# Adding expert results to the tokens' rows in DRAM, and transposing expert rows on VectorE, in an attention and mixture-of-experts block

## The chip, the cores and the metric

The kernel runs on one core of a Trainium2 chip. The metric is the device time of one execution in microseconds (us), as the median of several runs. The engines named below are TensorE (PE), VectorE (DVE), ScalarE (ACT), GpSimd (POOL) and SyncE (SP); SP, ACT and POOL also issue the DMAs.

## The reference

All tensors are float32. The input x has 4 batches of 512 tokens of 512 features, the context 4 batches of 1024 rows.

```python
def reference(x, ctx, Wq, Wg, bg, Wkv, Wo, Wr, We, be):
    # linear attention, 16 heads of 32 features, f(t) = t + 1 if t > 0 else exp(t)
    h = layernorm(x)
    q, gate = f(h @ Wq.T), sigmoid(h @ Wg.T + bg)
    k, v = split(ctx @ Wkv.T, 2);  k = f(k)
    kv, ks = einsum('bhsd,bhse->bhde', k, v), k.sum(over s)
    attn = einsum('bhld,bhde->bhle', q, kv) / (einsum('bhld,bhd->bhl', q, ks) + 1e-6)
    x = x + (attn * gate) @ Wo.T
    # mixture of experts: 8 experts, the best 2 for each token
    h = layernorm(x)
    w, sel = top_k(h @ Wr, 2);  w = softmax(w)
    gate[token, sel] = w                      # 0 for the other experts
    return x + sum over e of gate[..., e] * (h @ We[e] + be[e])
```

## The kernel before

The four batches go through attention one after another. While the projections of one batch run, the context tiles of the next are turned into keys and values (`kv_tiles`), so that TensorE has work throughout. All rows are tiles of 128 partitions.

After attention, `choose(b)` normalizes the four tiles of a batch into rows of `ROW` = 514 floats (512 features, the home row of the token, and the rank of its first expert), computes the routing logits and finds the two best experts. `dispatch(b)` counts the tokens of each expert and scatters each token's row twice into a DRAM tensor `stream`, which has one region for each expert. Each of the eight scatters of a batch (line 516) is an indirect DMA of GpSimd. `apart` tells the framework that scatters of a group need not wait for each other.

The rows of one expert are then read from `stream` in tiles of 128 tokens. A list says which expert and which rows tile j has; lists are computed on VectorE (`spans`, `listed`) and read into registers. The first 17 tiles (`EARLY`) are full of tokens of batches 0 to 2 and run beside the attention of batch 3; 18 more (`SURE`) always follow, and up to 4 come under a condition, which is not met here: 35 tiles run. `dispatch(3)` stands after the tenth early tile.

In `run`, `rows(j)` loads tile j (line 643, one DMA of 257 KB from SyncE), transposes it with four TensorE transposes (line 89) into PSUM, and ScalarE copies it back (line 231). `expert(j)` multiplies it by the expert's weights (line 86, tile `pe`), VectorE adds the bias into `y` (line 670), and GpSimd scatters `y` to the rows of a DRAM tensor `result` (line 681), where each of a token's two choices has a row of its own. So these scatters go under `apart`, too. `y` has three buffers, and tile j + 1 is loaded and transposed while tile j is multiplied.

At the end `fetch` reads the two result rows of each token back, `add` multiplies them by the gates and adds them to x in SBUF on VectorE (line 817), and `store` writes the output from ScalarE's queue. This is spread over the late tiles by a table of steps, `at_step`: batches 0 and 1 can be read once 8 late tiles are done (`DONE_2`), batch 2 after 14 (`DONE_3`), batch 3 at the end.

Order: the framework places instructions on each engine by when it expects them to be ready. `keep_in_program_order` fixes the order of matmuls and of some DMAs on their engines. It adds waits for what touches the same tensor, unless they are declared independent; a wait stands in the queue of the engine that issues, with all later work of that engine behind it.

Of the kernel before, what the change touches and what calls it, by code (L numbers as in the profile page):

```python
# [31 lines left out]
ROW = D + 2  # L32
# [16 lines left out]
def xattn_moe_kernel(  # L49
# [20 lines left out]
    xpool = ctx.enter_context(tc.tile_pool(name="x", bufs=B * NT))  # L70
# [11 lines left out]
    result = dram.tile([2 * TOK + LATE * P, F], F32, name="result")  # L82
# [8 lines left out]

    def load(dst, src):
        tc.keep_in_program_order(nc.sync.dma_start(out=dst, in_=src))

    def load_ctx(b, s):
        t = cpool.tile([P, ROW], F32, tag="cT", name=f"cT_{b}_{s}")
        t = t[:, 0:D].rearrange("p (c n) -> p c n", n=P)
        load(t, cT[b, s])
        return t
# [14 lines left out]
    bg_sb = wpool.tile([P, NC], F32, name="bg_sb")  # L114
    we_sb = wpool.tile([P, E, NC, F], F32, name="we_sb")

    ctx_tiles = {}

    first = cpool.tile([P, ROW], F32, tag="cT", name="cT_0_0")
    ctx_tiles[0, 0] = first[:, 0:D].rearrange("p (c n) -> p c n", n=P)  # L120
# [72 lines left out]
    home = numbers("home", [[2 * P, B * NT]], [P, B * NT], channel=2)  # L193
# [3 lines left out]
    nc.gpsimd.memset(empty[:, D : D + 1], float(2 * SLOTS))  # L197
    unread = numbers("unread", [[P, LATE]], [P, LATE], base=2 * TOK, channel=1)
# [88 lines left out]
    def kv_tiles(b, lo, hi, between=None, inside=None):  # L287
        for s in range(lo, hi):
            nxt = (b, s + 2) if s + 2 < NS else (b + 1, s + 2 - NS)
            if nxt[0] < B and nxt != (0, 2):  # L290
                ctx_tiles[nxt] = load_ctx(*nxt)
            if b in (1, 2) and s % 2 == 0:
                e = (b - 1) * E // 2 + s // 2
                load(we_sb[:, e], we[e])
            if (b, s) == (3, 0):
                load(stream[SLOTS : SLOTS + P, :], empty)
            if s == 0:
                sums[b] = pkv.tile([P, NC, 2 * P], F32, tag="kvs", name="kvs")
            k = made.pop(s) if s in made else keys(b, s)
            if (b, s) == (0, 0):  # L300
                made[1] = keys(0, 1)
            if inside is not None and s == lo:
                inside()
            v = values(b, s)
            if s > 0:
                kv_add(sums[b], s - 1, *pending[b])
            pending[b] = k, v
            if between is not None:
                between(s - lo)
# [91 lines left out]
    written = {"stream": [], "result": []}  # L401
# [17 lines left out]
    gates = const.tile([P, B * NT, 2], F32, name="gates")  # L419
# [5 lines left out]
    read_back = []  # L425
# [4 lines left out]
    def choose(b, mv, rstd):  # L430

        pl = pmm.tile([P, NT, E], F32, tag="mm", name="pl")
        rows, xTs = [], []
        for t in range(NT):
            row = work.tile([P, ROW], F32, tag="row", name="row", bufs=NT)
            normalize(row[:, 0:D], xs[b][t], t, mv, rstd)
            nc.gpsimd.tensor_copy(row[:, D : D + 1], home[:, b * NT + t : b * NT + t + 1])
            rows.append(row)
# [11 lines left out]
        for t in range(NT):  # L450
            xTs.append(work.tile([P, NC, P], F32, tag="z", name="x2T"))
            transposed(xTs[t], rows[t])
# [22 lines left out]
        routed[b] = rows, m1, hot1, first, m2, hot2  # L475
        yield

    def dispatch(b):

        rows, m1, hot1, first, m2, hot2 = routed.pop(b)  # L480
# [32 lines left out]
        for t in range(NT):  # L513
            nc.vector.tensor_copy(rows[t][:, D + 1 : D + 2], first[:, t, :])
            for i in range(2):
# [3 lines left out]
                    in_=rows[t],  # L519
# [6 lines left out]


        e2 = small.tile([P, NT, 1], F32, tag="e2", name="e2")
        w1 = gates[:, ts(b, NT), 0:1]
        nc.vector.tensor_tensor(e2, m2, m1, ALU.subtract)  # L530
        nc.scalar.activation(e2, e2, AF.Exp)
        nc.vector.tensor_scalar(w1, e2, 1.0, None, ALU.add)
        nc.vector.reciprocal(w1, w1)
        nc.vector.tensor_tensor(gates[:, ts(b, NT), 1:2], e2, w1, ALU.mult)
# [94 lines left out]
    def run(lists, lo, n, early):  # L629
# [3 lines left out]
        def rows(j):  # L633

            row = nc.values_load(
# [3 lines left out]
            if j % 5 < 3:  # L639
                xg = cpool.tile([P, ROW], F32, tag="cT", name="xg")  # L640
            else:
                xg = kvpool.tile([P, ROW], F32, tag="v", name="xg", bufs=2)
            load = nc.sync.dma_start(out=xg, in_=stream[ds(row, P), :])
            if early:
                behind(load, written["stream"][: 2 * NT * (B - 1)], "tokens of the tile")
                early_loads.append(load)
                for put in scatters.get(B - 1, []):
                    tc.declare_no_dep(load.ins, put.ins, reason=full_already)
            else:
                behind(load, written["stream"], "tokens of the tile")  # L650
            xT = work.tile([P, NC, P], F32, tag="qT", name="xgT", bufs=NC)
            transposed(xT, xg)
            return xT, xg

        def expert(j, xT, xg):
# [5 lines left out]
            for c in range(NC):  # L661
# [7 lines left out]
            y = kvpool.tile([P, F], F32, tag="k", name="y")  # L669
# [3 lines left out]
            home_i = small.tile([P, 1], U32, tag="to", name="to", bufs=8)  # L673

            at = small.tile([P, 1], F32, tag="at", name="at", bufs=8)
            nc.gpsimd.tensor_scalar(
                at, xg[:, D + 1 : D + 2], ranked[:, j : j + 1], xg[:, D : D + 1],
                ALU.is_equal, ALU.add,
            )
            nc.gpsimd.tensor_scalar(home_i, at, unread[:, j : j + 1], None, ALU.min)  # L680
            put = nc.gpsimd.indirect_dma_start(  # L681
                out=result,
                out_offset=bass.IndirectOffsetOnAxis(ap=home_i, axis=0),
                in_=y,
                in_offset=None,
            )
            apart(put, "result", "each choice has a row; rows without a token go unread")
            for got in read_back:
                tc.declare_no_dep(put.ins, got.ins, reason="no token of these is in the tile")

        ready = rows(lo)
        for j in range(lo, n):
            cur, ready = ready, rows(j + 1) if j + 1 < n else None
            expert(j, *cur)
# [8 lines left out]
    for b in range(B):  # L703
# [10 lines left out]
        if not more:  # L714
# [15 lines left out]
            early = run(early_list, 0, EARLY, True)  # L730
        product = products(qTs, z, aT)
# [52 lines left out]
    for e in range(E):  # L784
        row = nc.values_load(
            ends[0:1, e : e + 1], [ET.SP], min_val=0, max_val=SLOTS - P,
            skip_runtime_bounds_check_because="a region has room for all tokens",
        )
        fill = nc.sync.dma_start(out=stream[ds(row, P), :], in_=empty)
# [5 lines left out]
    flat = result[0 : 2 * TOK, :].rearrange("(t p i) f -> p t i f", p=P, i=2)  # L795
    homes = [(wpool, "wq"), (wpool, "wg"), (wpool, "wo"), (big, "xT"), (big, "aT")]
    fetched = {}

    def fetch(q, tiles):

        pool, tag = homes[q % len(homes)]
        yt = pool.tile([P, 2, 2, F], F32, tag=tag, name=f"y_{q}")
        for u in range(2):
            load = nc.sync.dma_start(out=yt[:, u], in_=flat[:, 2 * q + u])  # L804
            tc.keep_in_program_order(load)
            behind(load, written["result"][: EARLY + tiles], "results of the tokens")
            for put in written["result"][EARLY + tiles :]:
                tc.declare_no_dep(load.ins, put.ins, reason="no token of these is in the tile")
            read_back.append(load)
            fetched[2 * q + u] = yt[:, u]  # L810

    def add(t):
        xt = xs[t // NT][t % NT]
        yt = fetched[t]
        for i in range(2):
            tc.keep_in_program_order(
                nc.vector.scalar_tensor_tensor(  # L817
                    xt, yt[:, 1 - i, :], gates[:, t, i : i + 1], xt, ALU.mult, ALU.add
                )
            )  # L820

    def store(t):
        tc.keep_in_program_order(
            nc.scalar.dma_start(out=out[t // NT, t % NT], in_=xs[t // NT][t % NT])
        )

    at_step = {}
    first, last = 2 * NT, (B - 1) * NT
    for q in range(first // 2):
        at_step.setdefault(DONE_2 + 2 + q, []).append((fetch, q, DONE_2))  # L830
    for q in range(first // 2, last // 2):
        at_step.setdefault(DONE_3 + 2, []).append((fetch, q, DONE_3))
    for t in range(last):
        step = min(DONE_2 + 3 + t, SURE - 1 - (last - 5 - t) // 2)
        at_step.setdefault(step, []).append((add, t))
        at_step.setdefault(max(step + 1, DONE_2 + 5), []).append((store, t))

    def also(j):
        for what, *of in at_step.pop(j, []):
            what(*of)  # L840

    for j, _ in enumerate(run(late_list, 0, SURE, False)):
        also(j)
# [5 lines left out]
    with tc.If(many > SURE):  # L849
        for _ in run(late_list, SURE, SURE + 1, False):  # L850
            pass
        with tc.If(many > SURE + 1):
            for _ in run(late_list, SURE + 1, LATE, False):
                pass
    for j in sorted(at_step):
        also(j)
    for q in range(last // 2, TOK // P // 2):
        fetch(q, LATE)
    for t in range(last, TOK // P):
        add(t)  # L860
        store(t)
# [43 lines left out]
```

## Time and profile before

| what | value |
|---|---|
| median of 3 runs | 634.57 us (634.34 to 635.91) |
| profiled execution | 633.87 us |
| its span | 632.1 us |
| TensorE busy | 601.8 us, 95% of the span |
| VectorE, ScalarE, GpSimd busy | 235.9, 135.5, 108.5 us |
| mean granted TensorE clock | 0.984 |
| moved by DMA | 70.50 MB, 112 GB/s over the span |
| first and last scatter of a result | 457.58 and 613.52 us |

The span runs from the first to the last instruction of one execution taken by the hardware profiler; the time of that execution has some 1.8 us more. Engine rows give busy time. A group's row has its line, engine and operation, what it writes and reads, its number, its busy time and mean duration, and after the bar the idle time ahead of it and what ended that. A timeline row has start and duration in us, and in brackets the idle time before and its releaser. A DMA's landing is counted from its issue.

### The profile page before, as it was taken

To read this page: it belongs to the slowest core of one execution; us is meant where nothing else is said; L and a number is where in the kernel's file an instruction comes from. 1 tells how busy PE (TensorE), PEld (TensorE's weight loads), DVE (VectorE), ACT (ScalarE), POOL (GpSimd) and SP (SyncE) were. 2 spreads that over 40 slices of the span, in tenths; PEclk is the share of its full clock that TensorE was granted. 3 is DMA by queue.
4 is the path that set the end of the run, shared out by engine and by line. 5 is a ranking of instruction groups with operands and counts; after the bars stand their busy time and mean duration, and the time that the engine had idled before them with its cause. 6 is when DMAs were issued, how large, how long until landed. Compare 5 with 4: busy or idle time off the path is not lost. (4 is left out here: it accounts for less than half of the span.)

```text
span 632.1 us, 6250 instructions
## 1 busy us (share of the span) xinstructions
PE 601.8 (95%) x2044; PEld 300.1 (47%) x2044; DVE 235.9 (37%) x562; ACT 135.5 (21%) x215; POOL 108.5 (17%) x244
## 2 busy tenths in 40 slices
PE   7999999999999999999999999999999999999950
PEld 3555543544564345455543544664444654444420
DVE  3122244126234421622534135149424272111583
ACT  1322222113322122042222114322211221111100
POOL 3100000000005000000230000005331354743420
PEclk9999999999999999999999999999999999999985
DMA  8611300320243023022130100033431279647768
GB/s 316 184 34 54 130 0 7 112 83 18 85 165 117 18 83 109 9 98 89 48 116 18 34 17 17 1 133 135 117 117 33 84 217 238 212 135 255 286 256 284
DMA packets 27808, 70.50 MB, mean 112 GB/s; under 512 B 4288, under 2 KB 4800, under 8 KB 26368
## 3 DMA queue, kind: packets, MB, share of 16 engines
q1 hardware_dynamic: 19536, 48.04, 23.6%
q0 software_dynamic: 5360, 17.60, 7.7%
q10 hardware_dynamic: 2880, 4.46, 1.9%
q8 instruction: 17, 0.28, 0.2%
q14 instruction: 15, 0.12, 0.1%
HBM read 45.93 MB, written 24.16 MB: 111 GB/s over the span
## 5 line engine op out<-in xcount | busy, mean ns | idle before, releaser
L86 PE MATMUL pe<-we_sb,xgT 128*128 x280 | 125.8, 593 | 0.5 <-ACT xgT L231 0.5
L86 PE MATMUL pk<-wkv_sb,cT 128*128 128x512 f32 x256 | 117.8, 604 | 4.1 <-DMA wkv_sb<-in_wkv_dram 4.1
L86 PE MATMUL pv<-wkv_sb,cT 128*128 128x512 f32 x256 | 115.2, 594 | 0.0
L86 PEld LDWEIGHTS pv<-wkv_sb,cT 128*128 128x128 f32 x256 | 48.5, 190 | 62.2 <-issue 59.7
L206 DVE TENSOR_SCALAR ex<-pk 128x512 f32<-128x512 f32 x32 | 22.0, 689 | 147.4 <-PE pk L86 147.4
L86 PEld LDWEIGHTS pe<-we_sb,xgT 128*128 128x128 f32 x280 | 50.7, 190 | 52.1 <-issue 51.1
L86 PEld LDWEIGHTS pk<-wkv_sb,cT 128*128 128x128 f32 x256 | 47.5, 193 | 57.0 <-issue 50.1
L263 POOL MEMSET v<- 128x4 f32 x32 | 3.3, 104 | 344.7 <-PE kvs L86 281.8
L207 ACT ACTIVATE ex<-ex 128x512 f32<-128x512 f32 x48 | 30.2, 629 | 135.4 <-DVE ex L206 128.7
L86 PE MATMUL pg<-xT,wg_sb 128*128 128x512 f32 x128 | 56.7, 596 | 0.0
L86 PE MATMUL pq<-xT,wq_sb 128*128 128x512 f32 x128 | 56.6, 596 | 0.0
L670 DVE TENSOR_TENSOR y<-pe,be_sb 128x512 f32<-128x512 f32 x35 | 24.1, 690 | 85.2 <-PE pe L86 68.8
L86 PE MATMUL po<-wo_sb,aT 128*128 128x512 f32 x128 | 55.6, 592 | 0.0
L231 ACT COPY xgT<-pt 128x512 f32<-128x512 f32 x35 | 20.3, 585 | 120.2 <-PE pt L89 120.2
L681 POOL DMA_INDIRECT result<-y,to x35 | 37.4, 1069 | 36.7 <-DVE y L670 29.9
L516 POOL DMA_INDIRECT stream<-row,slot x32 | 32.1, 1002 | 49.6 <-DVE cmp L544 22.5
L86 PEld LDWEIGHTS kvs<-v,k 128*128 128x128 f32 x256 | 33.3, 191 | 13.4 <-issue 13.2
L86 PEld LDWEIGHTS pg<-xT,wg_sb 128*128 128x128 f32 x128 | 24.0, 190 | 32.0 <-issue 32.0
L86 PEld LDWEIGHTS po<-wo_sb,aT 128*128 128x128 f32 x128 | 24.1, 190 | 29.1 <-issue 28.9
L86 PEld LDWEIGHTS pq<-xT,wq_sb 128*128 128x128 f32 x128 | 23.8, 191 | 27.2 <-issue 27.2
L86 PE MATMUL kvs<-v,k 128*128 128x129 f32 x256 | 34.0, 275 | 0.0
L264 ACT COPY v<-pv 128x512 f32<-128x512 f32 x32 | 18.7, 584 | 53.5 <-PE pv L86 53.5
(151 smaller groups left out, 442.5 us busy)
## 6 DMA issues: line engine op xcount, KB each, us to landing
xg<-stream SPq DMA_DIRECT2D x35, 257.0 KB, 2.8
we_sb<-in_we_dram SPq DMA_DIRECT2D x8, 1024.0 KB, 5.0
y<-result SPq DMA_DIRECT2D x16, 512.0 KB, 7.3
cT<-in_cT_dram SPq DMA_DIRECT2D x31, 256.0 KB, 2.6
x<-in_x_dram SPq DMA_DIRECT2D x16, 256.0 KB, 4.2
out_dram<-x ACTq DMA_DIRECT2D x16, 256.0 KB, 2.8
stream<-empty SPq DMA_DIRECT2D x9, 257.0 KB, 6.9
wkv_sb<-in_wkv_dram SPq DMA_DIRECT2D x8, 256.0 KB, 4.6
```

The source lines that it names most:

```text
L86: tc.keep_in_program_order(nc.tensor.matmul(**operands))
L206: nc.vector.tensor_scalar(ex, src, 0.0, None, ALU.min)
L207: nc.scalar.activation(ex, ex, AF.Exp)
L231: nc.scalar.copy(dst, pt)
L263: nc.gpsimd.memset(v[:, :, P : P + 1], 1.0)
L264: nc.scalar.copy(v[:, :, 0:P], pv.rearrange("p (g f) -> p g f", f=P))
L516: put = nc.gpsimd.indirect_dma_start(out=stream, out_offset=bass.IndirectOffsetOnAxis(ap=slots[i][:, t, :], axis=0), in_=rows[t], in_offse ...
L670: nc.vector.tensor_tensor(y, pe, be_sb[:, ds(no, 1), :].rearrange("p o f -> p (o f)"), ALU.add)
L681: put = nc.gpsimd.indirect_dma_start(out=result, out_offset=bass.IndirectOffsetOnAxis(ap=home_i, axis=0), in_=y, in_offset=None,)
```

## The change

Seven things are done.

- The row of a token carries four extra floats in place of two: its token number, the rank of its first expert, the gate of the second and the difference of the two gates. The gates are computed in `choose` instead of `dispatch`. The four rows of a batch share one tile.
- `result` is replaced by `total`, a DRAM tensor with one row for each token and a tile of spare rows. `choose` stores x after attention there, from ScalarE's queue; x then has 8 tiles in SBUF instead of 16.
- After the bias, ScalarE multiplies `y` by the gate of each token. GpSimd scatters `y` with an addition onto the rows of `total`. These scatters are not declared independent of one another.
- The output leaves by DMA from `total` to the output tensor: batches 0 and 1 after late tile 11, batch 2 after late tile 17, batch 3 at the end in four parts on two queues.
- Rows of an expert are loaded by four DMAs, each of which puts 128 features of all 128 tokens on 32 partitions, and a fifth for the four extra floats. VectorE transposes the tile in 32x32 blocks. The expert weights are laid out to match, so each expert's weights come in four DMAs.
- Loads run five tiles ahead and transposes three; `y` has seven buffers.
- The eight fills behind the streams are issued by ScalarE instead of SyncE.

```diff
-ROW = D + 2
+ROW = D + 4
-    xpool = ctx.enter_context(tc.tile_pool(name="x", bufs=B * NT))
+    xpool = ctx.enter_context(tc.tile_pool(name="x", bufs=2 * NT))
-    result = dram.tile([2 * TOK + LATE * P, F], F32, name="result")
+    total = dram.tile([TOK + P, D], F32, name="total")
...
+    we_rows = we.rearrange("e (c f) i n -> e i f c n", f=HD)
...
-                load(we_sb[:, e], we[e])
+                for i in range(NC):
+                    load(we_sb[ts(i, HD), e], we_rows[e, i])
...
-        rows, xTs = [], []
+        rows = work.tile([P, NT, ROW], F32, tag="row", name="rows", bufs=1)
+        xTs = []
         for t in range(NT):
...
+            normalize(rows[:, t, 0:D], xs[b][t], t, mv, rstd)
+            token = (b * NT + t) * P
+            tc.keep_in_program_order(
+                nc.scalar.dma_start(out=total[token : token + P, :], in_=xs[b][t])
+            )
...
-            load = nc.sync.dma_start(out=xg, in_=stream[ds(row, P), :])
...
+            rows_of = stream[ds(row, P), :]
+            parts = []
+            for i in range(NC):
+                parts.append(
+                    (
+                        xg[ts(i, HD), :].rearrange("t (j f) -> t j f", j=NC),
+                        rows_of[:, ts(i, P)].rearrange("(j t) f -> t j f", t=HD),
+                    )
+                )
+            parts.append((of, rows_of[:, D:ROW]))
+            for dst, src in parts:
+                load = nc.sync.dma_start(out=dst, in_=src)
...
-            transposed(xT, xg)
...
+            nc.gpsimd.tensor_scalar(
+                weight, of[:, 1:2], ranked[:, j : j + 1], of[:, 3:4], ALU.is_equal, ALU.mult
+            )
+            nc.gpsimd.tensor_tensor(weight, weight, of[:, 2:3], ALU.add)
+            token = small.tile([P, 1], U32, tag="token", name="token", bufs=8)
+            nc.gpsimd.tensor_scalar(token, of[:, 0:1], unread, None, ALU.min)
+            xT = work.tile([P, NC, P], F32, tag="xgT", name="xgT", bufs=NC)
+            latest["turn"] = nc.vector.transpose(
+                xT.rearrange("p c (j t) -> p j c t", t=HD),
+                xg.rearrange("p (j c f) -> p j c f", j=NC, f=HD),
+            )
...
-            y = kvpool.tile([P, F], F32, tag="k", name="y")
+            tag, bufs = ("k", 3) if j % 7 < 3 else ("y", 4)
+            y = kvpool.tile([P, F], F32, tag=tag, name="y", bufs=bufs)
...
+            nc.scalar.activation(y, y, AF.Copy, scale=weight)
             put = nc.gpsimd.indirect_dma_start(
-                out=result,
-                out_offset=bass.IndirectOffsetOnAxis(ap=home_i, axis=0),
+                out=total,
+                out_offset=bass.IndirectOffsetOnAxis(ap=token, axis=0),
                 in_=y,
                 in_offset=None,
-            )
-            apart(put, "result", "each choice has a row; rows without a token go unread")
-            for got in read_back:
+                compute_op=ALU.add,
+            )
+            added.append(put)
+            for got in finished:
                 tc.declare_no_dep(put.ins, got.ins, reason="no token of these is in the tile")
...
+        def ahead(j):
+            if j + 5 < n:
+                with tc.issue_after(latest["load"].ins) if latest else nullcontext():
+                    loaded.append(rows(j + 5))
+            if j + 3 >= lo and loaded:
+                ready.append(turned(j + 3, *loaded.pop(0)))
+
+        for j in range(lo - 5, lo):
+            ahead(j)
+        yield
         for j in range(lo, n):
-            cur, ready = ready, rows(j + 1) if j + 1 < n else None
-            expert(j, *cur)
+            ahead(j)
+            with tc.issue_after(latest["turn"].ins):
+                expert(j, *ready.pop(0))
             yield
...
-        fill = nc.sync.dma_start(out=stream[ds(row, P), :], in_=empty)
+        fill = nc.scalar.dma_start(out=stream[ds(row, P), :], in_=empty)
...
+    def leave(b, queue, parts=1):
+        n = L // parts
+        for i in range(parts):
+            r = slice(b * L + i * n, b * L + (i + 1) * n)
+            done = queue[i % len(queue)].dma_start(
+                out=out[b].rearrange("t p d -> (t p) d")[i * n : (i + 1) * n], in_=total[r, :]
+            )
+            tc.keep_in_program_order(done)
+            finished.append(done)
+        latest["load"] = done
+
+    late = run(late_list, 0, SURE, False)
+    next(late)
+    for j, _ in enumerate(late):
+        if j == DONE_2 + 3:
+            leave(0, [nc.sync])
+            leave(1, [nc.sync])
+        if j == DONE_3 + 3:
+            leave(2, [nc.sync])
...
+    leave(B - 1, [nc.sync, nc.scalar], 4)
```

`DONE_2` is 8, `DONE_3` is 14 and `SURE` is 18.

More of the change, by code (lines that the diff above doesn't have):

```diff
@@ L1 @@
-from contextlib import ExitStack
+from contextlib import ExitStack, nullcontext
 import concourse.bass as bass
@@ L89, in transpose @@
         tc.keep_in_program_order(nc.tensor.transpose(dst, src, ident))
+    latest = {}
     def load(dst, src):
-        tc.keep_in_program_order(nc.sync.dma_start(out=dst, in_=src))
+        latest["load"] = nc.sync.dma_start(out=dst, in_=src)
+        tc.keep_in_program_order(latest["load"])
     def load_ctx(b, s):
-        t = cpool.tile([P, ROW], F32, tag="cT", name=f"cT_{b}_{s}")
-        t = t[:, 0:D].rearrange("p (c n) -> p c n", n=P)
+        t = cpool.tile([P, NC, P], F32, tag="cT", name=f"cT_{b}_{s}")
         load(t, cT[b, s])
@@ L115, in xattn_moe_kernel @@
     we_sb = wpool.tile([P, E, NC, F], F32, name="we_sb")
+    we_rows = we.rearrange("e (c f) i n -> e i f c n", f=HD)
     ctx_tiles = {}
-    first = cpool.tile([P, ROW], F32, tag="cT", name="cT_0_0")
-    ctx_tiles[0, 0] = first[:, 0:D].rearrange("p (c n) -> p c n", n=P)
+    ctx_tiles[0, 0] = cpool.tile([P, NC, P], F32, tag="cT", name="cT_0_0")
     for half in range(2):
@@ L191, in numbers @@
         return t
-    home = numbers("home", [[2 * P, B * NT]], [P, B * NT], channel=2)
+    home = numbers("home", [[P, B * NT]], [P, B * NT], channel=1)
     empty = const.tile([P, ROW], F32, name="empty")
     nc.gpsimd.memset(empty, 0.0)
-    nc.gpsimd.memset(empty[:, D : D + 1], float(2 * SLOTS))
-    unread = numbers("unread", [[P, LATE]], [P, LATE], base=2 * TOK, channel=1)
+    nc.gpsimd.memset(empty[:, D : D + 1], float(SLOTS))
+    unread = numbers("unread", [[0, 1]], [P, 1], base=TOK, channel=1)
     expert_no = numbers("expert_no", [[0, GROUPS], [1, E]], [P, GROUPS, E])
@@ L293, in kv_tiles @@
                 e = (b - 1) * E // 2 + s // 2
-                load(we_sb[:, e], we[e])
+                for i in range(NC):
+                    load(we_sb[ts(i, HD), e], we_rows[e, i])
             if (b, s) == (3, 0):
                 load(stream[SLOTS : SLOTS + P, :], empty)
+                load(total[TOK : TOK + P, :], empty[:, 0:D])
             if s == 0:
@@ L398, in attention_out @@
             nc.vector.tensor_tensor(xs[b][t], po, xs[b][t], ALU.add)
-    written = {"stream": [], "result": []}
+    written = {"stream": []}
     def apart(dma, group, why):
@@ L417, in behind @@
             )
-    gates = const.tile([P, B * NT, 2], F32, name="gates")
     seen = {0: const.tile([P, E], F32, name="seen")}
@@ L424, in xattn_moe_kernel @@
     early_loads = []
-    read_back = []
+    added, finished = [], []
     full_already = "the tile is full of tokens of other batches"
@@ L432, in choose @@
         pl = pmm.tile([P, NT, E], F32, tag="mm", name="pl")
-        rows, xTs = [], []
+        rows = work.tile([P, NT, ROW], F32, tag="row", name="rows", bufs=1)
+        xTs = []
         for t in range(NT):
[L435 to L438, printed above, removed]
+            normalize(rows[:, t, 0:D], xs[b][t], t, mv, rstd)
[3 more added lines that the diff above has]
+            )
+        nc.gpsimd.tensor_copy(
+            rows[:, :, D : D + 1], home[:, ts(b, NT)].rearrange("p (t o) -> p t o", o=1)
+        )
         def logits(t):
@@ L451, in choose @@
             xTs.append(work.tile([P, NC, P], F32, tag="z", name="x2T"))
-            transposed(xTs[t], rows[t])
+            transposed(xTs[t], rows[:, t, :])
             if t > 0:
@@ L473, in choose @@
         m2, hot2, _ = largest("2")
-        routed[b] = rows, m1, hot1, first, m2, hot2
+        e2 = small.tile([P, NT, 1], F32, tag="e2", name="e2")
+        w1 = small.tile([P, NT, 1], F32, tag="w1", name="w1")
+        nc.vector.tensor_tensor(e2, m2, m1, ALU.subtract)
+        nc.scalar.activation(e2, e2, AF.Exp)
+        nc.vector.tensor_scalar(w1, e2, 1.0, None, ALU.add)
+        nc.vector.reciprocal(w1, w1)
+        nc.vector.tensor_copy(rows[:, :, D + 1 : D + 2], first)
+        nc.vector.tensor_tensor(rows[:, :, D + 2 : D + 3], e2, w1, ALU.mult)
+        nc.vector.tensor_tensor(
+            rows[:, :, D + 3 : D + 4], w1, rows[:, :, D + 2 : D + 3], ALU.subtract
+        )
+        routed[b] = rows, hot1, hot2
         yield
     def dispatch(b):
-        rows, m1, hot1, first, m2, hot2 = routed.pop(b)
+        rows, hot1, hot2 = routed.pop(b)
         both = small.tile([P, NT, E], F32, tag="both", name="both")
@@ L513, in dispatch @@
         for t in range(NT):
-            nc.vector.tensor_copy(rows[t][:, D + 1 : D + 2], first[:, t, :])
             for i in range(2):
@@ L518, in dispatch @@
                     out_offset=bass.IndirectOffsetOnAxis(ap=slots[i][:, t, :], axis=0),
-                    in_=rows[t],
+                    in_=rows[:, t, :],
                     in_offset=None,
@@ L525, in dispatch @@
                 scatters[b].append(put)
[L528 to L534, printed above, removed]
     def per_expert(name):
@@ L639, in rows @@
             if j % 5 < 3:
-                xg = cpool.tile([P, ROW], F32, tag="cT", name="xg")
+                xg = cpool.tile([P, D], F32, tag="cT", name="xg")
             else:
-                xg = kvpool.tile([P, ROW], F32, tag="v", name="xg", bufs=2)
-            load = nc.sync.dma_start(out=xg, in_=stream[ds(row, P), :])
[L644 to L650, printed above, removed]
@@ L651, in rows @@
-            xT = work.tile([P, NC, P], F32, tag="qT", name="xgT", bufs=NC)
-            transposed(xT, xg)
-            return xT, xg
-        def expert(j, xT, xg):
+                xg = kvpool.tile([P, D], F32, tag="v", name="xg", bufs=2)
+            of = small.tile([P, ROW - D], F32, tag="of", name="of", bufs=8)
+            rows_of = stream[ds(row, P), :]
[7 more added lines that the diff above has]
+                )
@@ new lines, in rows @@
+            parts.append((of, rows_of[:, D:ROW]))
+            for dst, src in parts:
+                load = nc.sync.dma_start(out=dst, in_=src)
+                latest["load"] = load
+                if early:
+                    behind(load, written["stream"][: 2 * NT * (B - 1)], "tokens of the tile")
+                    early_loads.append(load)
+                    for put in scatters.get(B - 1, []):
+                        tc.declare_no_dep(load.ins, put.ins, reason=full_already)
+                else:
+                    behind(load, written["stream"], "tokens of the tile")
@@ new lines, in rows, with turned @@
+            return xg, of
+        def turned(j, xg, of):
+            weight = small.tile([P, 1], F32, tag="weight", name="weight", bufs=8)
+            nc.gpsimd.tensor_scalar(
[9 more added lines that the diff above has]
+            )
+            return xT, weight, token
@@ L656, in expert @@
+        def expert(j, xT, weight, token):
             no = nc.values_load(
@@ L672, in expert @@
             )
[L673 to L678, printed above, removed]
-            )
-            nc.gpsimd.tensor_scalar(home_i, at, unread[:, j : j + 1], None, ALU.min)
+            nc.scalar.activation(y, y, AF.Copy, scale=weight)
             put = nc.gpsimd.indirect_dma_start(
-                out=result,
-                out_offset=bass.IndirectOffsetOnAxis(ap=home_i, axis=0),
+                out=total,
+                out_offset=bass.IndirectOffsetOnAxis(ap=token, axis=0),
                 in_=y,
                 in_offset=None,
+                compute_op=ALU.add,
             )
-            apart(put, "result", "each choice has a row; rows without a token go unread")
-            for got in read_back:
+            added.append(put)
+            for got in finished:
                 tc.declare_no_dep(put.ins, got.ins, reason="no token of these is in the tile")
-        ready = rows(lo)
+        loaded, ready = [], []
+        def ahead(j):
[7 more added lines that the diff above has]
+        yield
         for j in range(lo, n):
-            cur, ready = ready, rows(j + 1) if j + 1 < n else None
-            expert(j, *cur)
+            ahead(j)
+            with tc.issue_after(latest["turn"].ins):
+                expert(j, *ready.pop(0))
             yield
@@ L730, in xattn_moe_kernel @@
             early = run(early_list, 0, EARLY, True)
+            next(early)
         product = products(qTs, z, aT)
@@ L785, in xattn_moe_kernel @@
         row = nc.values_load(
-            ends[0:1, e : e + 1], [ET.SP], min_val=0, max_val=SLOTS - P,
+            ends[0:1, e : e + 1], [ET.Activation], min_val=0, max_val=SLOTS - P,
             skip_runtime_bounds_check_because="a region has room for all tokens",
         )
-        fill = nc.sync.dma_start(out=stream[ds(row, P), :], in_=empty)
+        fill = nc.scalar.dma_start(out=stream[ds(row, P), :], in_=empty)
         apart(fill, "stream", "rows behind the last token of a stream")
@@ L792, in xattn_moe_kernel @@
             tc.declare_no_dep(fill.ins, load.ins, reason="behind all tokens of the stream")
[L795 to L819, printed above, removed]
-            )
[L822 to L840, printed above, removed]
@@ L842, in xattn_moe_kernel @@
-    for j, _ in enumerate(run(late_list, 0, SURE, False)):
-        also(j)
+    def leave(b, queue, parts=1):
[4 more added lines that the diff above has]
+                out=out[b].rearrange("t p d -> (t p) d")[i * n : (i + 1) * n], in_=total[r, :]
+            )
+            tc.keep_in_program_order(done)
+            finished.append(done)
+        latest["load"] = done
@@ L849, in xattn_moe_kernel @@
     with tc.If(many > SURE):
+        latest.clear()
         for _ in run(late_list, SURE, SURE + 1, False):
@@ L852, in xattn_moe_kernel @@
         with tc.If(many > SURE + 1):
+            latest.clear()
             for _ in run(late_list, SURE + 1, LATE, False):
                 pass
[L855 to L861, printed above, removed]
+    leave(B - 1, [nc.sync, nc.scalar], 4)
 def kernel(**inputs):
```

## The prediction

> **What bounds the kernel now.** I read the page first, for the engine that sets the time, then the groups by line and shape, TensorE's timeline of the expert stage, GpSimd's timeline of the same stage, the scatter's own line, and the chain that ended last.
>
> ```profile
> PE 601.8 (95%) x2044; PEld 300.1 (47%) x2044; DVE 235.9 (37%) x562; ACT 135.5 (21%) x215; POOL 108.5 (17%) x244
> ...
> q0 software_dynamic: 5360, 17.60, 7.7%
> ...
> xg<-stream SPq DMA_DIRECT2D x35, 257.0 KB, 2.8
> ...
> result<-y,to POOLq DMA_INDIRECT x35, 3.6
> ```
>
> TensorE is busy for 95% of the span, so work taken off it counts, unless something else takes its place. A scatter lands 3.6 us (median) after its issue. The scatters' queue q0 takes 7.7% of the span on each DMA engine: 0.077 x 632.1 / 67 scatters (35 + 32) = 0.73 us of moving data per scatter; the rest of the 3.6 us is fixed.
>
> TensorE in the late stage, one expert tile after another:
>
> ```profile
> 571.05 0.60 PE L89 MATMUL pt<-ident,xg 128*128 128x128 f32 x4
> 571.49 3.60 PE L86 MATMUL pe<-we_sb,xgT 128*128 x8
> 574.92 0.60 PE L89 MATMUL pt<-ident,xg 128*128 128x128 f32 x4
> 575.36 3.60 PE L86 MATMUL pe<-we_sb,xgT 128*128 x8
> ```
>
> The period is 574.92 - 571.05 = 3.87 us: 0.44 us of transposes and 3.43 us of expert matmuls. The engine doesn't stop between tiles.
>
> GpSimd around the last routing step (512.96 is the tenth result scatter, 525.24 the eleventh):
>
> ```profile
> 512.96 1.07 POOL L681 DMA_INDIRECT result<-y,to  x1 [0.81 <-DVE counts L503]
> 514.35 0.96 POOL L516 DMA_INDIRECT stream<-row,slot  x1 [0.32 <-DVE ends L783]
> ...
> 523.98 0.96 POOL L516 DMA_INDIRECT stream<-row,slot  x1 [0.30 <-issue]
> 525.24 0.96 POOL L681 DMA_INDIRECT result<-y,to  x1 [0.30 <-DVE y L670]
> 526.23 0.41 POOL L676 TENSOR_SCALAR at<-xg,rankedA 128x1 f32<-128x1 f32 x1
> ...
> 527.42 1.07 POOL L681 DMA_INDIRECT result<-y,to  x1 [0.40 <-issue]
> 528.79 0.96 POOL L681 DMA_INDIRECT result<-y,to  x1 [0.30 <-issue]
> ```
>
> The result scatters of before may overlap: 527.42 and 528.79 start 1.4 us apart, though one needs about 3 us to land. Eight stream scatters hold the queue for 8 x 1.27 = 10.2 us. The scatter's line gives the spread of its landing:
>
> ```profile
> DMA to landing us min/median/max: 2.8/3.6/8.6
> ```
>
> And the end of the chain:
>
> ```profile
> 613.52 2.93 DMA result<-y,to
> ...
> 616.63 4.76 DMA y<-result
> 621.40 0.02 issue
> 621.41 5.73 DMA y<-result
> ```
>
> Last scatter 2.93 us, the reads of the results 10.5 us, then adds and a store: the tail from the last matmul (602.47 + 7.03 = 609.5) to 632.1 is 22.6 us.
>
> **The change part by part.**
>
> *Transposes leave TensorE.* 35 tiles x 0.435 us = 15.2 us, on the bound engine. VectorE takes one 128x512 transpose per tile. The trace has none; the nearest rows of that shape in SBUF are 0.54 us (the normalizing of a row) and, as the dearest, 3.35 us (the reciprocal). I take 0.7: with the bias add (0.69) it is 1.4 of every 3.43 us, free. At 3.35 it would be 4.0 per tile, a new pace, but still under the 4.5 found below. The 32 gating adds (23.4 us) leave VectorE. ScalarE swaps a 0.585 us copy for a scaling of about 0.63.
>
> *Loads of expert rows.* One transfer per tile becomes five: 5 x 0.33 = 1.7 us of issue on SyncE per 3.43 us, five tiles ahead. The Trainium skill (DMA: Bandwidth & Descriptors, "Rules for kernel authors") speaks against this: transfers under 64 KB pay mostly overhead and should be merged. If the five paid one after another, 5 x 2.8 = 14 us per tile, the loads would set a pace of 14 us. But in the row of before, issues go out without waiting for landings, and the lead of five tiles is 17 us, so I count nothing. The cover is that lead.
>
> *Result rows, gates and final adds go; a scatter with an addition takes their place.* The old scatters were declared independent of each other. The new ones are not, and all address the same tensor through run-time indices, so each must wait, at the head of GpSimd's queue, until the one before has landed. Queued behind it there are the weights of the tile three ahead (three small operations, about 1.3 us, which fit into the flight) and the stream scatters. The new price is the link T, from one start to the next.
> Low end: 2.8 us, the fastest landing without any addition. High end: 7.2, a read and a write in turn at 3.6 each. The row alone gives 3.6 + 0.15 for waking up (its neighbours show 0.02 to 0.30) = 3.75. The Trainium skill (Collectives: The Full Stack, "The bandwidth ceiling: the fold count and why AG ≠ RS ≠ AR") says that an addition in the DMA engine is slow because it needs two source reads, which halves its rate; that doubles the 0.73: T = 3.6 + 0.73 + 0.15 = 4.5. No run here shows it yet. I take 4.5, near the row; both T exceed TensorE's 3.43.
>
> *Stores of x into the total* (16 issues of 0.34 us on ScalarE, 21% busy) replace the output stores. For batch 3 they come after six scatter-adds and must wait for them, with ScalarE's queue behind them; scatter-add 7 waits for them. ScalarE's stall may hold the routing copies and so TensorE for up to some 5 us; that is covered by the backlog of scatters, and would cost its length if there were none.
>
> *Fills on ScalarE*, eight, as long as on SyncE (9.8 us): they hold up some scalings around 514 to 524, when GpSimd is busy with stream scatters; nothing. *Weight loads in quarters, routing weights made earlier, fewer x buffers*: SyncE and VectorE wait for TensorE there; nothing.
>
> *Leaving.* Batches 0 and 1 leave after late tile 11; batch 2 is placed at late tile 17, the last, so it waits for the last scatter-add as batch 3 does. 2 MB then go from DRAM to DRAM. The stage of 575 to 590 us moved 345 GB/s, the tail 277: 2.1 MB at 300 is 7 us, plus 2.8 to land = 10; at half the rate for both sides in DRAM it is 17. I take 11.
>
> **The sum, with T = 4.5.** The first four additions come early (457 to 475) and are done before the fifth. Fifth at 486.5, sixth at 491, landed 495.5; stores 4 x 0.34 + 2.8 = 4.2, so the seventh is at 499.8, then 504.3, 508.8, 513.3 (the tenth). TensorE has the routing of batch 3 at about 510, so the stream scatters follow at once: 513.3 + 1.07 + 10.2 = 524.6 for the eleventh. From there 25 links x 4.5 = 112.5, to 637.1. In the flood of stream rows and fills the landing was 6.4 instead of 3.6 (525 to 540 us): add 4. Batches 0 and 1 leaving: add 4. Last addition landed at 645.1; 11 for leaving: span 656. The profiled execution took 633.87 with a span of 632.1, so 1.8 lie around it; the median of the runs is 634.57, 0.7 above that execution. 656.1 + 1.8 + 0.7 = 658.6.
> TensorE alone would be done at 609.5 - 15.2 = 594, so it waits for free y buffers (seven) instead. One microsecond more in T is about 30 us in the end.
>
> **The rivals.**
> *The addition is almost free (faster).* T = 3.0, as the last scatter of before (2.93). The same list then gives 603 for the last landing and 616.7 in the end. For it: 2.8 to 2.9 in quiet stretches. Against it: 3.6 with normal traffic, and an addition can't cost less than a write. It decides below T = 3.65, where the list gives 634.
> *The scatters are not serial after all.* Then TensorE's end at 594, 1.4 for add and scaling, 3.6 and 11, plus 2.5, give about 613. Against it: nothing in the diff declares the additions independent, only the leaving batches.
> *The addition is dear.* [...]T = 6 gives 704, 7.2 gives 740. For it: nothing in the trace; no row excludes it.
>
> **How the numbers follow.** A measurement of this kernel can tell about 0.3% (1.9 us) from no change. Chain at T of 3.72 to 5.55: 0.69, likeliest 658.6. Dearer: 0.13. T near 3.65 (within 1.9 us): 0.04. Cheaper addition: 0.10; not serial: 0.04. So faster 0.14, same 0.04, slower 0.82. The range goes from T = 3.6 (632) to 5.55 (690), leaving out about 0.1 at each end.
>
> **What would show it.** Right: GpSimd's scatter waits for the DMA of the scatter before, a start every 4 to 5 us from about 500 us on with only the stream scatters between; TensorE idle in the late stage; L89 transposes of xg gone; the chain made of scatters, then one DRAM copy. Wrong: starts 3.4 us apart with TensorE's 3.43 us period unbroken (the faster case), over 5.5 us apart, or waits for xg or a VectorE transpose of over 2.7 us setting the pace.

## The result, and the profile after

The changed kernel takes 692.02 us (median of 4 runs, 691.89 to 693.15), the kernel before 634.46 beside it: a ratio of 1.0907 (95% interval 1.0886 to 1.0928). It is slower, as forecast, but by 57.6 us where 24 were forecast, and it lies just above the range. The profiled execution has a span of 690.2 us.

The page of the changed kernel, busy time and the queue of the scatters:

```profile
PE 596.5 (86%) x1904; PEld 289.2 (42%) x1904; DVE 234.3 (34%) x557; ACT 140.3 (20%) x215; POOL 130.4 (19%) x267
...
q0 software_dynamic: 7600, 17.63, 13.4%
...
L89 PE MATMUL pe<-we_sb,xgT 128*128 x280 | 130.9, 625 | 53.2 <-DVE xgT L693 53.2
...
L719 POOL DMA_INDIRECT total<-y,token x35 | 56.5, 1615 | 102.9 <-DMA total<-y,token 77.4
```

TensorE has lost its place as the bound: 86% busy instead of 95%, and idle for 53.2 us ahead of expert matmuls. The scatter's row names the new one. GpSimd stood 102.9 us ahead of its 35 scatters, 77.4 of them until the addition before had landed. The queue q0 moves the same 17.6 MB, but in 7600 packets instead of 5360, and for 13.4% of the span instead of 7.7%. If the 32 stream scatters still cost 0.73 us each, an addition takes (0.134 x 690.2 - 32 x 0.73) / 35 = 1.97 us of every DMA engine, 2.7 times a plain scatter. TensorE's busy time fell by 5.3 us only, though 15.2 us of transposes are gone; its mean granted clock is 0.941 instead of 0.984, and the expert matmuls take 625 ns on average instead of 593.

The chain that ended last, in order of time:

```profile
597.45 0.02 issue
597.47 0.02 POOLq L719
597.49 0.69 issue
598.18 4.81 DMA total<-y,token
```

This pattern repeats to the end: an addition lands 4.7 to 5.0 us after its issue, but for one of 9.6, and 0.7 us go by until GpSimd issues the next. The starts themselves, in GpSimd's timeline (the first two are the sixth and seventh addition, then come the 14th, the 21st and 22nd, and the 30th and 31st):

```profile
493.58 1.62 POOL L719 DMA_INDIRECT total<-y,token  x1 [0.16 <-issue]
...
503.83 1.63 POOL L719 DMA_INDIRECT total<-y,token  x1 [1.57 <-DMA total<-x]
...
550.39 1.62 POOL L719 DMA_INDIRECT total<-y,token  x1 [3.55 <-issue]
...
592.47 1.62 POOL L719 DMA_INDIRECT total<-y,token  x1 [2.95 <-DMA total<-y,token]
...
598.18 1.62 POOL L719 DMA_INDIRECT total<-y,token  x1 [3.09 <-DMA total<-y,token]
...
643.05 1.55 POOL L719 DMA_INDIRECT total<-y,token  x1 [4.03 <-DMA total<-y,token]
653.41 1.53 POOL L719 DMA_INDIRECT total<-y,token  x1 [8.81 <-DMA total<-y,token]
```

From 592.47 to 643.05 the links are 5.45 to 5.7 us, most of them over the 5.5 that the prediction names as a sign of being wrong. TensorE's timeline at the end shows how little its own work matters:

```profile
575.33 34.60 PE L89 MATMUL pe<-we_sb,xgT 128*128 x80 [2.81 <-DVE xgT L693]
610.12 3.70 PE L89 MATMUL pe<-we_sb,xgT 128*128 x8 [0.19 <-DVE xgT L693]
654.39 6.37 PE L89 MATMUL pe<-we_sb,xgT 128*128 x8 [40.58 <-DVE xgT L693]
```

It stands for 40.6 us ahead of the last tile, whose load is behind the leaving batches 0 and 1 on SyncE. Even that is covered: earlier results are still waiting for their additions, and the last addition starts only at 675.67.

### The profile page after: what moved, and what is told of

It is laid out like the page before. It is cut to its first block, busy times and chain, and to the rows that moved or that the text cites. A ratio compares the mean times of both kernels' runs of the same rounds, so it can differ in the third digit from the quotient of the medians.

```text
span 690.2 us, 6460 instructions
## 1 busy us (share of the span) xinstructions
PE 596.5 (86%) x1904; PEld 289.2 (42%) x1904; DVE 234.3 (34%) x557; ACT 140.3 (20%) x215; POOL 130.4 (19%) x267
## 3 DMA queue, kind: packets, MB, share of 16 engines
q0 software_dynamic: 7600, 17.63, 13.4%
## 5 line engine op out<-in xcount | busy, mean ns | idle before, releaser
L89 PE MATMUL pe<-we_sb,xgT 128*128 x280 | 130.9, 625 | 53.2 <-DVE xgT L693 53.2
L89 PEld LDWEIGHTS pe<-we_sb,xgT 128*128 128x128 f32 x280 | 55.1, 201 | 125.8 <-issue 64.6
L719 POOL DMA_INDIRECT total<-y,token x35 | 56.5, 1615 | 102.9 <-DMA total<-y,token 77.4
L718 ACT ACTIVATE y<-y,weight 128x512 f32<-128x512 f32 x35 | 25.1, 722 | 166.0 <-DVE y L715 70.5
L693 DVE STREAM_TRANSPOSE xgT<-xg 128x512 f32<-128x512 f32 x35 | 24.6, 703 | 68.4 <-SPq L873 38.5
L540 POOL DMA_INDIRECT stream<-rows,slot x32 | 31.8, 992 | 49.5 <-DVE cmp L559 22.5
L89 PEld LDWEIGHTS kvs<-v,k 128*128 128x128 f32 x256 | 33.3, 191 | 13.4 <-issue 13.4
```

The lines of the kernel that those rows point to most:

```text
L89: tc.keep_in_program_order(nc.tensor.matmul(**operands))
L540: put = nc.gpsimd.indirect_dma_start(out=stream, out_offset=bass.IndirectOffsetOnAxis(ap=slots[i][:, t, :], axis=0), in_=rows[:, t, :], in ...
L693: latest["turn"] = nc.vector.transpose(xT.rearrange("p c (j t) -> p j c t", t=HD), xg.rearrange("p (j c f) -> p j c f", j=NC, f=HD),)
L718: nc.scalar.activation(y, y, AF.Copy, scale=weight)
L719: put = nc.gpsimd.indirect_dma_start(out=total, out_offset=bass.IndirectOffsetOnAxis(ap=token, axis=0), in_=y, in_offset=None, compute_op= ...
```

## The experiments

The theory to test, A: the additions form a chain, and the addition itself makes the link long. Its main rival, B: the link is long because of the waiting and the traffic of the split loads, and would be without any addition. And where did TensorE's 15 us go?

**The chain without the addition.**

```diff
-                compute_op=ALU.add,
```

> The changed kernel with the addition taken out of the scatters, which still wait for one another: each row of the total keeps what was written last, so the sums are left out. Theory A (the addition lengthens each link of the chain): GpSimd takes about 1.07 us instead of 1.62 for a scatter, the landing falls from 4.9 to about 3.1, the link from 5.6 to about 3.9 us, and the time from 692 to about 645. Rival B (the wait and the 512-byte pieces of the loads make the link long, the addition does not): link 5 us or more, time 675 or more.

632.18 us; 0.9957 times before (0.9941 to 0.9973). Starts from its GpSimd timeline (the 14th, 18th, 19th and 30th scatter):

```profile
534.30 1.08 POOL L719 DMA_INDIRECT total<-y,token  x1 [1.62 <-issue]
...
550.26 1.08 POOL L719 DMA_INDIRECT total<-y,token  x1 [0.97 <-issue]
...
554.03 1.08 POOL L719 DMA_INDIRECT total<-y,token  x1 [1.82 <-DMA total<-y,token]
...
595.02 0.96 POOL L719 DMA_INDIRECT total<-y,token  x1 [2.45 <-DMA total<-y,token]
```

From the 14th to the 30th scatter a link is (595.02 - 534.30) / 16 = 3.80 us, in the changed kernel (643.05 - 550.39) / 16 = 5.79: 2.0 us less, times some 30 links, is the 60 us between the two kernels. The last scatter starts at 618.66 instead of 675.67, so 57 of the 60 us lie ahead of it. GpSimd's part falls to 1.08 us. The waits and the split loads are all still there, so B is out as the reason for the long link. The time came out 13 us under the estimate of 645.

**Two chains.** Two totals take turns (16 stores of zeros for the second one are left out here):

```diff
-                out=total,
+                out=(total, total_b)[len(added) % 2],
```

> The changed kernel with two total tensors: even tiles are added to the first, odd tiles to the second (set to zero by 16 further DMAs), so that there are two chains side by side. The additions of the odd tiles are left out of the output. Theory A (the length of one chain sets the end): two links run at once, 2.8 to 3.2 us for each tile, less than TensorE's 3.43, so TensorE's stage is unbroken again and the time is 613 to 630. Rival (the additions are bound by the DMA engines or by GpSimd's queue, not by their waiting for one another): starts stay over 4.5 us apart, time over 655.

640.61 us (1.0095; 1.0064 to 1.0125). The chain no longer sets the pace, but the time is 10 us above the expectation. TensorE shows the reason:

```profile
540.20 58.63 PE L90 MATMUL pe<-we_sb,xgT 128*128 x136 [3.13 <-DVE xgT L698]
613.91 5.11 PE L90 MATMUL pe<-we_sb,xgT 128*128 x8 [15.08 <-DVE xgT L698]
```

The matmuls of 17 late tiles follow one another, 3.45 us each, and then TensorE stands for 15 us for the last tile, whose load SyncE issues behind the leaving batches. So I moved these behind that load:

```diff
-        if j == DONE_2 + 3:
+        if j == DONE_2 + 5:
```

> As with two total tensors (the additions of odd tiles left out of the output), but batches 0 and 1 leave after late tile 13 instead of 11, behind the load of the last tile. There TensorE stood still for 15 us, for a tile whose load stood behind the leaving batches on SyncE, which wait for additions. If that was what held the end, 12 to 15 us come off: 626 to 629. If the end is set by the additions or by leaving, no change: 638 to 642.

636.73 us (1.0036; 1.0027 to 1.0045). The stop is gone, but only 4 of the 12 to 15 us come off. The last additions, with the leaving batches beside them, are late instead:

```profile
607.97 1.54 POOL L724 DMA_INDIRECT total<-y,token  x1 [2.00 <-DMA total<-y,token]
610.18 1.54 POOL L724 DMA_INDIRECT total_b<-y,token  x1 [0.68 <-DMA total_b<-y,token]
619.82 1.54 POOL L724 DMA_INDIRECT total<-y,token  x1 [8.09 <-DMA total<-y,token]
```

The last of all waits for one that took 11.1 us to land; SyncE had issued the leaving batches 0 and 1 at 607.25, just before that one. The stop was thus one part of what held the end. That these bulk transfers are another is read from the trace and was not tried.

**Transposes back on TensorE**, with whole loads and the old layout of the weights:

```diff
+            parts = [(xg, rows_of[:, 0:D])]
...
-            latest["turn"] = nc.vector.transpose(
-                xT.rearrange("p c (j t) -> p j c t", t=HD),
-                xg.rearrange("p (j c f) -> p j c f", j=NC, f=HD),
-            )
+            transposed(xT, xg)
```

> The changed kernel with the transposes back on TensorE and expert rows loaded whole (one DMA of 256 KB and the small one), everything else kept. Theory A (only the chain counts): TensorE's 15 us come back but lie beside the chain; link 5.6, time 688 to 697. Rival B (the 512-byte pieces of the loads slow the additions): link under 5.0, time under 675. Rival C (waits for VectorE's transposes take part in the loss): over 5 us faster.

697.03 us (1.0979; 1.0956 to 1.1001), at the edge of theory A's 688 to 697, and most links from 5.3 to 5.9 us. From the 14th to the 30th addition a link is 5.63 us instead of 5.79, so the loads in 512-byte pieces don't make it long, nor do VectorE's transposes have a part in the loss. TensorE's 15 us lie beside the chain but for 5. The starts of the fifth and the eighth addition show where these are lost:

```profile
492.35 1.63 POOL L708 DMA_INDIRECT total<-y,token  x1 [9.47 <-ACT y L707]
...
516.26 1.60 POOL L708 DMA_INDIRECT total<-y,token  x1 [2.46 <-ACT y L707]
```

They come 4.4 and 7.2 us later than in the changed kernel (487.94 and 509.05), and both waited for their scaled `y`. There the additions have no backlog yet, so GpSimd waits for the tile itself. At the last addition the lag is 6.3 us, no more than at the eighth.

**The scatters by themselves**, in a kernel that does nothing else:

```diff
+    for i in range(N):
+        put(plain, False)
+    for i in range(N):
+        put(adds, True)
+    for i in range(N):
+        put(half, True, D // 2)
...
```

> Scatters of one 128x512 tile by themselves on an otherwise quiet chip, ten in a row of each kind, nothing else of the reference computed (the output is a copy of x): plain ones chained, additions chained, additions of half rows (128x256) chained, plain ones to ten tensors, additions to ten tensors, and additions chained beside 160 loads of 64 KB in 512-byte pieces. Theory A (the addition costs GpSimd 0.55 us and the DMA engines 1.2 us): starts 3.5, 5.5, about 4.9, 1.4 and 1.9 us apart (the last held by the DMA engines at 2.0), and no more than 1 us longer beside the loads. Rival B (traffic makes the link): additions chained on the quiet chip under 4.5 us apart, over 5.5 beside the loads.

GpSimd's timeline, one start of each chained kind (plain, additions, half rows) and one of the additions to different tensors:

```profile
48.02 0.97 POOL L51 DMA_INDIRECT plain<-y,token  x1 [2.02 <-DMA plain<-y,token]
...
92.87 1.55 POOL L51 DMA_INDIRECT adds<-y,token  x1 [3.62 <-DMA adds<-y,token]
...
132.60 1.55 POOL L51 DMA_INDIRECT half<-y,token  x1 [2.52 <-DMA half<-y,token]
...
166.21 1.55 POOL L51 DMA_INDIRECT aa<-y,token  x1 [0.30 <-issue]
```

Links, as means of the series in one execution: 3.0 us plain, 5.1 for additions, 4.1 for half the row; unchained additions start 1.87 us apart, which is GpSimd's 1.55 and a gap of 0.30. (The first four plain links overlap the filling of the tensors with zeros and are left aside.) The first three expectations were up to 0.8 us too high; the differences between the kinds are what the theory needs. On a quiet chip, too, an addition costs 2.1 us more than a plain scatter: 0.58 on GpSimd (1.55 for 0.97) and 1.5 until it has landed. The row of the queue in three stretches shows where these 1.5 are spent (four plain scatters in 39.06 to 50.99, eight additions in 57.57 to 97.91, eight of half rows in 104.38 to 136.66):

```profile
q0 software_dynamic: 320, 1.05, 23.0%
q0 software_dynamic: 1152, 2.10, 43.3%
q0 software_dynamic: 1152, 1.05, 29.0%
```

Per scatter that is 80 packets and 0.69 us of every DMA engine for plain ones (0.230 x 11.93 / 4), 144 packets and 2.18 us for additions, 144 packets and 1.17 us for half rows. So the addition costs the DMA engines 1.5 us more, as the link says, and half the bytes save the same 1.0 us here and there.

Beside 64 KB loads the starts are 5.2 to 6.3 us apart, up to 1.2 more than the mean without loads and 5.6 on average, where at most 1 more was expected. Part of the difference between 5.1 here and 5.6 to 5.8 in the changed kernel lies elsewhere: after a landing GpSimd starts the next scatter 0.27 us later here, and 0.7 us later there. What it does in the rest of that time the traces don't show.

**The waiting alone**, in the kernel before:

```diff
-            apart(put, "result", "each choice has a row; rows without a token go unread")
+            written["result"].append(put)
```

> The kernel before with its plain result scatters no longer declared independent, so that each waits for the one before; nothing else changes. If a plain link is 3.8 us, as without the addition in the changed kernel, it is just under TensorE's period of 3.87 here, and only the stream scatters and the crowded stretches are made up for late: 634 to 645. If the waiting by itself were the loss (rival B): 660 or more.

653.61 us (1.0293; 1.0276 to 1.0309), above the expectation but under rival B's 660. From the eleventh scatter on most links are short enough, 3.4 to 4.0 us. Six are not: 7.6 and 5.2 behind the stream scatters, 5.0 at 561.72, 8.1 at 618.37, and the two that follow here:

```profile
584.58 1.07 POOL L681 DMA_INDIRECT result<-y,to  x1 [1.66 <-DMA result<-y,to]
588.14 1.07 POOL L681 DMA_INDIRECT result<-y,to  x1 [1.66 <-DMA result<-y,to]
596.32 0.96 POOL L681 DMA_INDIRECT result<-y,to  x1 [7.11 <-DMA result<-y,to]
603.28 0.96 POOL L681 DMA_INDIRECT result<-y,to  x1 [6.00 <-DMA result<-y,to]
```

3.56 us between the first pair, then 8.2 and 7.0 while eight reads of 512 KB, which SyncE issued from 587.4, go by. In the kernel before, where scatters may overlap, the starts beside the same reads (issued from 575.35) stay 3.87 us apart up to 587.71; only the next one comes 6.6 later. So waiting alone does cost 19 us in a kernel that reads results back beside its chain. The changed kernel reads none back, so these 19 us can't be carried over to it.

**The transposes alone**, on the kernel before: the five loads, the layout of the weights and VectorE's transpose, with result rows and gates as they were. For want of room the turned rows take one of the five buffers for reading back.

```diff
+            slots_of["xgT"] = big.tile([P, NC, NC, P], F32, tag="xT", name="xgT")
...
-            transposed(xT, xg)
+            latest["turn"] = nc.vector.transpose(
+                xT.rearrange("p c (j t) -> p j c t", t=HD),
+                xg[:, 0:D].rearrange("p (j c f) -> p j c f", j=NC, f=HD),
+            )
```

> The kernel before with only the transposes moved to VectorE: loads of the expert rows in five DMAs, five tiles ahead, weights laid out to match; result rows, gates and final additions as before. Theory A: the 15.2 us of transposes leave the bound engine and nothing takes their place, so about 619 (615 to 624). Rival (the split loads or VectorE's queue cost what TensorE gains): 630 or more. The late results are read back into four buffers instead of five, worth at most 2 us.

635.8 us (1.0021; 1.0011 to 1.0032): nothing gained, where 619 was expected. TensorE did finish early, at 591.77 + 3.70 = 595.5 instead of 609.5. VectorE lost it again:

```profile
593.46 0.74 DVE L859 SCALAR_TENSOR_TENSOR x<-y,gates,x 128x512 f32<-128x512 f32 x1
603.29 2.74 DVE L859 SCALAR_TENSOR_TENSOR x<-y,gates,x 128x512 f32<-128x512 f32 x4 [9.09 <-DMA y<-result]
605.95 0.68 DVE L697 TENSOR_TENSOR y<-pe,be_sb 128x512 f32<-128x512 f32 x1
```

The bias of a tile that was long multiplied (L697) stands behind gated additions (L859), and these wait 9.1 us for rows being read back. The table of steps was made for a slower TensorE. So I moved the additions, with all else as in the run above:

```diff
-        step = min(DONE_2 + 3 + t, SURE - 1 - (last - 5 - t) // 2)
+        step = DONE_2 + 5 + t if t < NT else SURE + t
...
+    with tc.issue_after(last_y.ins):
```

> As with the transposes alone moved to VectorE, but the additions of the read-back results to x on VectorE come later: those of batch 0 from late tile 13 on, all others behind the bias of the last tile. There TensorE was done at 595.5 instead of 609.5, and then three biases stood on VectorE behind additions that waited for rows read back. If that ate the 14 us, this kernel takes 618 to 626. If the reading back is bound by the DMA engines anyway, 632 to 636.

629.89 us, 0.9926 times before (0.9912 to 0.9939): 0.7% faster than the kernel before, and 4 us short of the expectation. So the place of the additions held back some 6 of the 14 us. The last scatter starts at 603.37 instead of 614.46. What holds back the rest was not tried. In the trace biases now wait for a free y buffer, that is, for scatters that land late beside the reading:

```profile
597.83 0.69 DVE L697 TENSOR_TENSOR y<-pe,be_sb 128x512 f32<-128x512 f32 x1 [4.09 <-DMA result<-y,to]
```

## Why the prediction was wrong in size

*The chain: right.* The additions wait for one another, the link is longer than TensorE's period, and the starts from the fifth addition on set the end. Taking away the addition, or the single chain (with the leaving batches moved), takes away nearly all of the loss: 632 and 637 us, each within 0.5% of the kernel before.

*The addition's term in the link: the step that failed.* I wrote T = 3.6 + 0.73 + 0.15 = 4.5; measured are 5.79 us from the 14th to the 30th addition, and 5.45 to 5.7 in most later links. The plain part was good: 3.75 in the prediction, 3.80 in the chain without the addition. That was luck in part, since two errors cancel: some 0.7 us go by between a landing and the next start, not 0.15 (I had the neighbours of other instructions for it), and the landing in the chain is 3.1 (3.80 - 0.69), not 3.6. Nor is the rest of a landing fixed, as I had put it: a plain scatter lands after 2.7 us alone and 3.1 in that chain. The term that was mis-sized is the addition: 0.73 assumed, 2.0 measured (5.79 - 3.80). The Trainium skill's rule (Collectives: The Full Stack, "The bandwidth ceiling: the fold count and why AG ≠ RS ≠ AR"), two reads instead of one, made me double the data's time. The page speaks of a ring of collectives, and carrying it over to a scatter was my step; here it is 2.7 times, 1.97 for 0.73, and 3.2 times in the scatters by themselves, 2.18 for 0.69. And I had left out that GpSimd needs longer to issue an addition, 1.62 for 1.07 us. 0.55 + 1.24 = 1.8 of the 2.0 us. With 5.7 for T the list of the prediction (688.6 at 5.5, 30 us for each microsecond) ends at 694.6, against 692.0 measured. I had put the end of the range at 5.55.

*The other terms.* From the 10th to the 11th addition, across the stream scatters, 12.9 us against 11.3; for the eight of them I had put 8 x 1.27 = 10.2, while before they take 10.9 already (514.35 to 525.24), two of them being longer. The flood after it, for which I added 4, cost next to nothing: the next three links are 5.9. The stores of batch 3 put 10.25 us between the sixth and seventh addition, 4.5 above a link; 4.2 were forecast. Leaving of batches 0 and 1: one link of 10.4 us, 4.8 more than its neighbours; 4 forecast. From the last landing (680.5) to the end: 9.7, with 11 forecast. The five loads of a tile take SyncE 3.0 us with all that stands between them (first issues at 444.89 and 447.90), not 1.7, which is close to TensorE's 3.43 but far under the link. Four of the five are of 64.0 KB, so the prediction's words on transfers under 64 KB bear on the fifth alone, of 2 KB. With whole loads the links are 0.16 us shorter (5.63 for 5.79), so counting nothing for the split was close.

*TensorE.* Its 15.2 us lay under the chain, as the prediction said, and ScalarE's wait on the stores did stop it, 3.8 us ahead of the routing of batch 3, while the additions waited for the same stores. VectorE's transpose took 0.70 us, as assumed. What the prediction lacked is the 40.6 us stop for the last tile: I had named SyncE's queue for the issues of the loads, and not for the wait of the leaving batches ahead of one. Under the chain it was free. With two chains it was 15 us long, and taking it away saved 4.

*The faster rival.* With a chain at 3.8 us the end is at 632; the list gives 638 for that T, so it is some 5 us too long there. The rival of a scatter without waits (613) is not borne out where it could be tried: two chains still gave 637, and the transposes alone 636, or 630 with VectorE's additions moved. In the traces bulk transfers and queues behind them stand at the end of these runs. Additions without any waiting were not tried: two tiles can hold the same token.

## What to carry to other kernels

Before turning independent writes into dependent ones, work out the link: issue, landing, waking up and the cost of the operation that makes them dependent; compare it with the period of the stage, and multiply the difference by the number of links. Size an operation that the trace lacks by measuring it alone, chained and unchained, before arguing from a ratio. When a bound engine gets faster, look at once at what was timed to its old pace: here hand-placed steps kept the whole gain of the transposes from showing, and moving them brought back a part.

## What the hardware showed that I had not expected

- A scatter with an addition of 256 KB onto rows in DRAM held the DMA engines for 1.97 us in the changed kernel and 2.18 us on the quiet chip, in 144 packets ((7600 - 32 x 80) / 35), a plain one for 0.73 and 0.69 us, in 80 packets. GpSimd takes 1.62 instead of 1.07 us to issue it. Half rows take as many packets and 1.17 us.
- Between the landing of one scatter and GpSimd's start of the next, 0.7 us passed in the chains of the large kernels and 0.27 us in the scatters by themselves; unchained scatters have 0.30 us between them.
- A link beside bulk transfers was about twice as long: 10.4 instead of 5.6 us beside 2 MB from DRAM to DRAM, 8.2 instead of 3.6 beside eight reads of 512 KB.
